# Blending a deformable-convolution sample: two VectorE operations in a row, one ScalarE scaling after them, and TensorE a tap later

## The chip, the cores and the metric

The kernel runs on one core of a Trainium2 chip. The metric is the device time of one execution in microseconds; the time before is the median of three runs. All profiles are of one execution of the kernel, recorded by the hardware profiler. The recorded execution is longer than the timed ones (7982.62 us against 7477.65 us), so shares and differences are read from the profile and times from the timed runs.

## The reference

Four images of 256 channels and 64x64 positions go through a normalisation over channels, three layers of modulated deformable 3x3 convolution with a ReLU each, a residual, and then a mixture of experts (two of eight for each token) with another residual. The change concerns the sampling in the deformable layers:

```python
y0 = jnp.floor(ys); x0 = jnp.floor(xs)
wy = (ys - y0)[:, None]; wx = (xs - x0)[:, None]
...
return v00 * (1 - wy) * (1 - wx) + v01 * (1 - wy) * wx + v10 * wy * (1 - wx) + v11 * wy * wx
...
sampled = _bilinear(x, ys, xs) * mask[:, None]      # mask = sigmoid(...)
out = jnp.einsum('bikhw,oik->bohw', sampled, wk) + b[None, :, None, None]
x = jax.nn.relu(out)                                 # three such layers
```

Each output position thus needs nine samples (the taps of the 3x3 kernel), each sample four neighbours weighted by the fractions wy and wx and by a mask.

## The kernel before

A table in DRAM holds for every position the row of 256 channel values and the difference to the row below it, so that one gather of 1024 numbers per position brings the left and the right column, each as (value, difference). The work goes in blocks of 512 positions: 4 groups of 128 positions (the partitions), times 9 taps, are 36 samples of 128x256. There are 96 blocks and so 3456 samples. For a tap `k` the loop treats the four groups in two pairs:

```python
def main_block(self, i, n, wins):
    ...
    acc = self.ps1.tile([P, CC, BLK], F32, tag="acc", ...)
    for k in range(K):
        sT = self.smT.tile([P, CC, BLK], F32, tag="sT", ...)
        for t0 in range(0, TPB, 2):
            tp = self.ps.tile([P, CC, 2 * P], F32, tag="tp", ...)
            gs, ss = [], []
            for t in (t0, t0 + 1):
                j = t * K + k
                g = self.gat.tile([P, 2, 2, C], F32, tag="g", ...)      # 10 buffers
                nc.gpsimd.indirect_dma_start(out=g..., in_=tb, in_offset=...)          # L445
                nc.vector.scalar_tensor_tensor(                                       # L451
                    g[:, :, 0, :], g[:, :, 1, :], cf[:, j, 0:1], g[:, :, 0, :], ALU.mult, ALU.add)
                s = self.smp.tile([P, C], F32, tag="s", ...)            # 6 buffers
                nc.scalar.activation(s, g[:, 0, 0, :], AF.Copy, scale=cf[:, j, 1:2])   # L456
                gs.append(g); ss.append(s)
            for u in range(2):
                j = (t0 + u) * K + k
                nc.vector.scalar_tensor_tensor(                                       # L461
                    ss[u], gs[u][:, 1, 0, :], cf[:, j, 2:3], ss[u], ALU.mult, ALU.add)
                for c in range(CC):
                    nc.tensor.transpose(tp[:, c, u*P:(u+1)*P], ss[u][:, c*P:(c+1)*P], self.ident)  # L465
            nc.scalar.copy(sT[:, :, t0 * P : (t0 + 2) * P], tp)                       # L470
        self.finish()                        # the matmuls of the tap before: acc += wk * sT  (L488)
        self.pend = (i, n, k, acc, sT, wins)
        self.step(k)                         # a piece of side work: tables, offsets, tokens
        self.pump()                          # a piece of the experts
```

L451 blends the rows of both columns at once (128x512 elements): value + wy * difference. L456 scales the left column by `(1 - wx) * mask` on ScalarE, and L461 adds the right column times `wx * mask` on VectorE. TensorE transposes the sample (L465), ScalarE copies the transposed pair from PSUM to SBUF (L470), and TensorE accumulates the tap (L488).

The three coefficients of a sample are made once for a block (the mask is `(1 + tanh)/2`):

```python
nc.vector.tensor_copy(cf[:, :, 0], fr[:, 0, :])                               # wy
for q, (s0, s1) in enumerate(((-0.5, 0.5), (0.5, 0.0))):
    hf = small(f"hf{q}", (P, J))
    nc.vector.tensor_scalar(hf, fr[:, 1, :], s0, s1, ALU.mult, ALU.add)       # (1-wx)/2, wx/2
    nc.vector.scalar_tensor_tensor(cf[:, :, 1 + q], th, 1.0, hf, ALU.add, ALU.mult)
```

The experts run beside the sampling: GpSimd's queue, which issues the gathers in order, also issues the load of an expert's weights (`w`, two buffers, L727) and of its tokens. The instructions of each engine are put in order by a scheduler when the program is built; an engine executes its own in that order.

Of the kernel before, what the change touches and what calls it, by code (L numbers as in the profile page):

```python
# [8 lines left out]
F32 = mybir.dt.float32  # L9
I32 = mybir.dt.int32  # L10
AF = mybir.ActivationFunctionType
ALU = mybir.AluOpType
AX = mybir.AxisListType

P = 128
H = W = 64
C = 256
CC = C // P
K = 9
NL = 3  # L20
TPB = 4
BLK = P * TPB
NB = H * W // BLK
RPB = BLK // W
J = TPB * K
# [10 lines left out]
FT = 1 << FT_LOG  # L36
FU = FT // P
GB = 10
WINN = CC * (RPB + 2) * (W + 2)
W1N = CC * HID + HC  # L40
W2N = HC * C + C
# [43 lines left out]
class Weave:  # L85
# [3 lines left out]
    def __init__(self, ctx, tc, ins, out):  # L89
        nc = self.nc = tc.nc  # L90
        self.tc = tc
        self.ins = ins
        self.x = ins["x"].rearrange("b (c p) h w -> b p c (h w)", p=P)
        self.out_v = out.rearrange("b (c p) h w -> b p c (h w)", p=P)
        self.B = self.x.shape[0]

        def pool(name, bufs, **kw):
            return ctx.enter_context(tc.tile_pool(name=name, bufs=bufs, **kw))

        self.cst = pool("cst", 1)  # L100
        self.dram = pool("dram", 1, space=bass.MemoryType.DRAM)
        self.wkp = pool("wkp", 1)
        self.plan = pool("plan", 22)
        self.win = pool("win", 3)
        self.wt = pool("wt", 2)
        self.small = pool("small", 1)
        self.big = pool("big", 2)
        self.ffn = pool("ffn", 2)
        self.rt = pool("rt", 1)
        self.rt2 = pool("rt2", 2)  # L110
        self.gyp = pool("gyp", 4)
        self.smT = pool("smT", 2)
        self.smp = pool("smp", 6)
        self.gat = pool("gat", GB)
        self.ps = pool("ps", 3, space=bass.MemoryType.PSUM)
        self.ps1 = pool("ps1", 1, space=bass.MemoryType.PSUM)
        self.queue = []
        self.credit = 0.0
        self.side = []
        self.tiles = []  # L120
        self.tile_credit = 0.0
        self.pend = None

# [108 lines left out]
    def window(self, n, nm, spare):  # L234

        if spare:
            if n % 2 == 0:
                self.pair = self.wt.tile([P, 2, WINN], F32, tag="wt", name=f"win_{nm}")
            w = self.pair[:, n % 2, :].rearrange("p (c r w) -> p c r w", c=CC, w=W + 2)
        else:  # L240
            w = self.win.tile([P, CC, RPB + 2, W + 2], F32, tag="win", name=f"win_{nm}")
        v = w.rearrange("p c r w -> p (c r) w")
        self.nc.vector.memset(v[:, :, 0 : W + 2 : W + 1], 0.0)
        if n == 0:
            self.nc.vector.memset(w[:, :, 0, 1 : W + 1], 0.0)
        if n == NB - 1:
            self.nc.vector.memset(w[:, :, RPB + 1, 1 : W + 1], 0.0)
        return w
# [61 lines left out]
    def off_block(self, l, b, n, w):  # L310

        nc = self.nc
        nm = f"{l}_{b}_{n}"
# [4 lines left out]
        for m, (k, c) in enumerate(terms):  # L318
            ky, kx = divmod(k, 3)
            g = m % NQ  # L320
# [22 lines left out]
        def small(tag, shape=(P, 2, J), dt=F32):  # L343
            return self.small.tile(list(shape), dt, tag=tag, name=f"{tag}_{nm}")

        idx = self.plan.tile([P, J], I32, tag="idx", name=f"idx_{nm}")
        cf = self.plan.tile([P, J, 3], F32, tag="cf", name=f"cf_{nm}")
        self.plans[l, b, n] = (idx, cf)

        th = small("th", (P, J))  # L350
# [22 lines left out]
        fr = small("fr")  # L373
# [5 lines left out]
        nc.vector.tensor_scalar(idx, ixf, float(TC + 1), None, ALU.add)  # L379
        yield  # L380

        nc.vector.tensor_copy(cf[:, :, 0], fr[:, 0, :])
        for q, (s0, s1) in enumerate(((-0.5, 0.5), (0.5, 0.0))):
            hf = small(f"hf{q}", (P, J))
            nc.vector.tensor_scalar(hf, fr[:, 1, :], s0, s1, ALU.mult, ALU.add)
            nc.vector.scalar_tensor_tensor(cf[:, :, 1 + q], th, 1.0, hf, ALU.add, ALU.mult)

    def pre_block(self, b, n, wins, spare):

# [38 lines left out]
        self.wk[k] = wk  # L428

    def main_block(self, i, n, wins):  # L430
        nc = self.nc
        l, b = self.stages[i]
        nm = f"{i}_{n}"
        idx, cf = self.plans.pop((l, b, n))
        tb = self.table(l, b)
        acc = self.ps1.tile([P, CC, BLK], F32, tag="acc", name=f"acc_{nm}")
        for k in range(K):
            sT = self.smT.tile([P, CC, BLK], F32, tag="sT", name=f"sT_{nm}_{k}")
            for t0 in range(0, TPB, 2):
                tp = self.ps.tile([P, CC, 2 * P], F32, tag="tp", name=f"tp_{nm}_{k}_{t0}")  # L440
                gs, ss = [], []
                for t in (t0, t0 + 1):
                    j = t * K + k
                    g = self.gat.tile([P, 2, 2, C], F32, tag="g", name=f"g_{nm}_{j}")
                    nc.gpsimd.indirect_dma_start(  # L445
                        out=g.rearrange("p x s f -> p (x s f)"),
                        out_offset=None,
                        in_=tb,
                        in_offset=bass.IndirectOffsetOnAxis(ap=idx[:, j : j + 1], axis=0),
                    )  # L450
                    nc.vector.scalar_tensor_tensor(  # L451
                        g[:, :, 0, :], g[:, :, 1, :], cf[:, j, 0:1], g[:, :, 0, :],
                        ALU.mult, ALU.add,
                    )
                    s = self.smp.tile([P, C], F32, tag="s", name=f"s_{nm}_{j}")
                    nc.scalar.activation(s, g[:, 0, 0, :], AF.Copy, scale=cf[:, j, 1:2])  # L456
                    gs.append(g)
                    ss.append(s)
                for u in range(2):
                    j = (t0 + u) * K + k  # L460
                    nc.vector.scalar_tensor_tensor(  # L461
                        ss[u], gs[u][:, 1, 0, :], cf[:, j, 2:3], ss[u], ALU.mult, ALU.add
                    )
                    for c in range(CC):
                        nc.tensor.transpose(  # L465
                            tp[:, c, u * P : (u + 1) * P],
                            ss[u][:, c * P : (c + 1) * P],
                            self.ident,
                        )
                nc.scalar.copy(sT[:, :, t0 * P : (t0 + 2) * P], tp)  # L470

            self.finish()
            self.pend = (i, n, k, acc, sT, wins)
            self.step(k)
            self.pump()

    def finish(self):

        if self.pend is None:
            return  # L480
        nc = self.nc
        i, n, k, acc, sT, wins = self.pend
        self.pend = None
        l, b = self.stages[i]
        nm = f"{i}_{n}"
        for o in range(CC):
            for c in range(CC):
                nc.tensor.matmul(  # L488
                    acc[:, o, :],
                    lhsT=self.wk[k][:, c, o * P : (o + 1) * P],  # L490
                    rhs=sT[:, c, :],
                    start=(k == 0 and c == 0),
                    stop=(k == K - 1 and c == CC - 1),
                )
        if n == NB - 1 and i + 1 < len(self.stages):
            self.load_tap(self.stages[i + 1][0], k, i + 1)
        if k < K - 1:
            return
        bk = self.bk[l]
        if l < NL - 1:  # L500
            w = wins[n] = self.window(n, nm, False)
            dst = [w[:, o, 1 : RPB + 1, 1 : W + 1] for o in range(CC)]
            src = [acc[:, o, :].rearrange("p (r w) -> p r w", w=W) for o in range(CC)]
        else:
            r = self.big.tile([P, CC, BLK], F32, tag="a", name=f"r_{nm}")
            dst = [r[:, o, :] for o in range(CC)]
            src = [acc[:, o, :] for o in range(CC)]
        nc.scalar.activation(dst[0], src[0], AF.Relu, bias=bk[:, 0:1])
        nc.vector.tensor_scalar(dst[1], src[1], bk[:, 1:2], 0.0, ALU.add, ALU.max)
        if l < NL - 1:  # L510
            self.rows_done(l + 1, b, n, wins)
        else:
            self.aside(5, self.tokens(b, n, r))
# [382 lines left out]
    def run(self):  # L896
# [14 lines left out]
        wins = {}  # L911
# [6 lines left out]
        for i, (l, b) in enumerate(self.stages):  # L918
            wins, pre = {}, {}
            for n in range(NB):  # L920
                self.main_block(i, n, wins)
                if i in beside:
                    self.aside(3, self.pre_block(beside[i], n, pre, i == 0))
            if i + 1 == len(self.stages) or self.stages[i + 1] == (l + 1, b):
                self.finish()
                self.settle()
        while self.queue or self.tiles:
# [49 lines left out]
```

## Time and profile before

| | |
|---|---|
| Time, median of 3 runs | 7477.65 us (7471.17 to 7482.62) |
| Span of the profiled execution | 7980.6 us, 92242 instructions |
| TensorE (PE) busy, mean granted clock | 6750.9 us (85%), 0.939 |
| VectorE (DVE) busy | 5033.4 us (63%) |
| ScalarE (ACT) busy | 3584.0 us (45%) |
| GpSimd (POOL) busy | 4536.3 us (57%) |
| DMA | 2210.66 MB, mean 277 GB/s; the gathers' queue takes 68.8% of 16 engines' span |

How to read it: busy time is the time in which an engine executes something; the rest is idle time, and the profile names for each idle stretch what ended it. [...] "PEld" is TensorE's weight load. In a line such as `A x <- B y: us, times, longest`, engine A stood still before an instruction that writes x until engine B had made y. "issue" is idle time for which the profile shows no other engine. From about 7400 us on there are no samples left, only experts and the final combination.

### The profile page before, as it was taken

Reading aid. Unit: us, or ns where it says so; the run is one execution under the profiler, and the core shown is the slowest. Engines: PE = TensorE matmul, PEld = TensorE weight load, DVE = VectorE, ACT = ScalarE, POOL = GpSimd, SP = SyncE. Lnnn points to the kernel's source line nnn. Section 1 sums busy time; section 2 is a strip of 40 time slices with the busy share of each in tenths; the row PEclk is TensorE's granted clock in tenths of the full one; section 3 lists DMA queues with packets and bytes.
Section 4 is the critical chain, followed back from the end, with each engine's and each line's share of the span. In section 5 each row is a group of like instructions: output and inputs, shape, how many; then the busy total and the mean of one; then the engine's idle time right before and its main releaser. Section 6 shows DMA issues by size and latency. Waiting matters only on the chain. (4 is left out here: it accounts for less than half of the span.)

```text
span 7980.6 us, 92242 instructions
## 1 busy us (share of the span) xinstructions
PE 6750.9 (85%) x27544; PEld 3696.8 (46%) x27544; DVE 5033.4 (63%) x11300; ACT 3584.0 (45%) x7355; POOL 4536.3 (57%) x4189
## 2 busy tenths in 40 slices
PE   6898888888988999988887899998888788888595
PEld 2444333334444445445543454444444444555374
DVE  4776777768886666666666666666666445556401
ACT  3554454445544444445543444445453333444121
POOL 1664666665656666655555566666555544555434
PEclk8999999999999999999988999999998889999697
DMA  4897999899987888887787898888887666767423
GB/s 148 312 330 279 328 321 338 315 325 329 357 307 275 298 305 314 304 306 268 277 294 267 282 316 303 292 307 300 285 298 248 233 233 233 274 248 285 133 94 119
DMA packets 751193, 2210.66 MB, mean 277 GB/s; under 512 B 105688, under 2 KB 206040, under 8 KB 746088
## 3 DMA queue, kind: packets, MB, share of 16 engines
q0 software_dynamic: 547392, 1929.26, 68.8%
q1 hardware_dynamic: 203304, 275.51, 10.2%
q8 instruction: 222, 3.64, 0.2%
q14 instruction: 275, 2.25, 0.1%
HBM read 2150.57 MB, written 195.61 MB: 294 GB/s over the span
## 5 line engine op out<-in xcount | busy, mean ns | idle before, releaser
L445 POOL DMA_INDIRECT g<-tab,idx x3456 | 3754.0, 1086 | 2382.0 <-DVE s L461 1219.3
L488 PE MATMUL acc<-sT,wk 128*128 128x512 f32 x6912 | 3502.4, 625 | 267.2 <-ACT sT L470 165.9
L461 DVE SCALAR_TENSOR_TENSOR s<-g,cf,s 128x256 f32<-128x256 f32 x3456 | 1623.6, 482 | 1669.9 <-ACT s L456 1271.3
L451 DVE SCALAR_TENSOR_TENSOR g<-g,cf 128x512 f32<-128x512 f32 x3456 | 2519.3, 744 | 236.9 <-DMA g<-tab,idx 194.1
L456 ACT ACTIVATE s<-g,cf 128x256 f32<-128x256 f32 x3456 | 1691.8, 509 | 1159.6 <-DVE g L451 903.7
L488 PEld LDWEIGHTS acc<-sT,wk 128*128 128x128 f32 x6912 | 1216.3, 198 | 1270.5 <-issue 894.2
L470 ACT COPY sT<-tp 128x512 f32<-128x512 f32 x1728 | 1003.8, 585 | 1678.0 <-PE tp L465 1178.7
L465 PE MATMUL tp<-ident,s 128*128 128x128 f32 x6912 | 1302.0, 286 | 427.2 <-DVE s L461 271.5
L465 PEld LDWEIGHTS tp<-ident,s 128*128 128x128 f32 x6912 | 877.4, 146 | 1659.4 <-issue 1008.6
L791 PE MATMUL py<-w,hT 128*128 128x256 f32 x2496 | 689.3, 398 | 123.8 <-ACT hT L785 88.6
L775 PE MATMUL ph<-fzT,w 128*128 128x256 f32 x2496 | 661.3, 395 | 59.8 <-ACT hT L785 20.6
L791 PEld LDWEIGHTS py<-w,hT 128*128 128x128 f32 x2496 | 447.0, 195 | 271.6 <-ACT hT L785 137.4
L727 POOL DMA_INDIRECT w<-in_W,wrow x156 | 175.8, 1127 | 693.2 <-issue 260.5
L775 PEld LDWEIGHTS ph<-fzT,w 128*128 128x128 f32 x2496 | 463.5, 197 | 184.4 <-issue 74.1
L785 ACT ACTIVATE hT<-ph,w 128x256 f32<-128x256 f32 x624 | 268.7, 471 | 538.1 <-PE ph L775 270.8
L321 PE MATMUL po<-win,wo 128*32 128x512 f32 x2304 | 464.1, 614 | 49.2 <-ACT win L256 33.0
L739 POOL DMA_INDIRECT zt<-z,tok x312 | 347.6, 1114 | 140.7 <-issue 85.6
L820 POOL DMA_INDIRECT gy<-ys,slots x256 | 257.7, 1007 | 219.4 <-DVE ta L828 105.1
L799 DVE TENSOR_TENSOR y<-py,w 128x512 f32<-128x512 f32 x156 | 107.5, 689 | 341.4 <-PE py L791 331.8
L291 ACT COPY hv<-tpv 128x512 f32<-128x512 f32 x384 | 210.5, 595 | 99.1 <-PE tpv L286 56.7
L321 PE MATMUL po<-win_pre,wo 128*32 128x512 f32 x1152 | 227.6, 640 | 17.7 <-ACT om L330 7.9
L828 DVE SCALAR_TENSOR_TENSOR ta<-gy,cw,ta 128x256 f32<-128x256 f32 x256 | 120.5, 482 | 125.4 <-DMA gy<-ys,slots 84.7
(151 smaller groups left out, 3621.4 us busy)
## 6 DMA issues: line engine op xcount, KB each, us to landing
tab<-hv SPq DMA_DIRECT2D x384, 256.0 KB
g<-tab,idx POOLq DMA_INDIRECT x3456
ys<-y SPq DMA_DIRECT2D x156, 256.0 KB
wk<-in_conv_w SPq DMA_DIRECT2D x108, 256.0 KB
xc_pre<-in_x SPq DMA_DIRECT2D x32, 512.0 KB
xr_tok<-in_x SPq DMA_DIRECT2D x32, 512.0 KB
t<-t_tok SPq DMA_DIRECT2D x32, 512.0 KB
ta<-t SPq DMA_DIRECT2D x64, 256.0 KB
```

What stands on the lines that cost most here:

```text
L321: nc.tensor.matmul(po[g * Q : (g + 1) * Q, :], lhsT=self.wo[l][:, k, c, :], rhs=w[:, c, ky : ky + RPB, kx : kx + W], start=(m < NQ), stop= ...
L445: nc.gpsimd.indirect_dma_start(out=g.rearrange("p x s f -> p (x s f)"), out_offset=None, in_=tb, in_offset=bass.IndirectOffsetOnAxis(ap=id ...
L451: nc.vector.scalar_tensor_tensor(g[:, :, 0, :], g[:, :, 1, :], cf[:, j, 0:1], g[:, :, 0, :], ALU.mult, ALU.add,)
L456: nc.scalar.activation(s, g[:, 0, 0, :], AF.Copy, scale=cf[:, j, 1:2])
L461: nc.vector.scalar_tensor_tensor(ss[u], gs[u][:, 1, 0, :], cf[:, j, 2:3], ss[u], ALU.mult, ALU.add)
L465: nc.tensor.transpose(tp[:, c, u * P : (u + 1) * P], ss[u][:, c * P : (c + 1) * P], self.ident,)
L470: nc.scalar.copy(sT[:, :, t0 * P : (t0 + 2) * P], tp)
L488: nc.tensor.matmul(acc[:, o, :], lhsT=self.wk[k][:, c, o * P : (o + 1) * P], rhs=sT[:, c, :], start=(k == 0 and c == 0), stop=(k == K - 1 ...
L739: self.nc.gpsimd.indirect_dma_start(out=zt, out_offset=None, in_=grp.zd, in_offset=bass.IndirectOffsetOnAxis(ap=grp.tok[:, j : j + 1], axi ...
L775: nc.tensor.matmul(ph[:, h, :], lhsT=w1[:, o : o + P], rhs=zT[:, c, :], start=(c == 0), stop=(c == CC - 1),)
L785: nc.scalar.activation(ht[:, h, :], ph[:, h, :], AF.Gelu, bias=w1[:, k : k + 1])
L791: nc.tensor.matmul(py[:, u, :], lhsT=hT[h // 2][:, h % 2, u * P : (u + 1) * P], rhs=w2[:, h * C : (h + 1) * C], start=(h == 0), stop=(h == ...
```

## The change

A sample becomes `((left + ratio * right)) * scale` with `ratio = wx / (1 - wx)` and `scale = (1 - wx) * mask`. VectorE then makes both blends one after the other without anything of ScalarE between them, and ScalarE's scaling comes last, in place. `1 - wx` is kept at or above 2^-30 so that the ratio stays finite. TensorE's part of a pair (its transposes, the copy of the result, and the tap's matmuls) is put two pairs (one tap) later in the program, and the samples have eight buffers instead of six. The purpose is that VectorE never has to wait in the middle of a sample, that the gather buffer is given back after two consecutive VectorE operations, and that TensorE finds its samples ready.

```diff
+LAG = 2
+LEAST = 2.0**-30
...
-        self.smp = pool("smp", 6)
+        self.smp = pool("smp", 8)
...
         nc.vector.tensor_copy(cf[:, :, 0], fr[:, 0, :])
-        for q, (s0, s1) in enumerate(((-0.5, 0.5), (0.5, 0.0))):
-            hf = small(f"hf{q}", (P, J))
-            nc.vector.tensor_scalar(hf, fr[:, 1, :], s0, s1, ALU.mult, ALU.add)
-            nc.vector.scalar_tensor_tensor(cf[:, :, 1 + q], th, 1.0, hf, ALU.add, ALU.mult)
+        left = small("left", (P, J))
+        nc.vector.tensor_scalar(left, fr[:, 1, :], -1.0, 1.0, ALU.mult, ALU.add)
+        nc.vector.tensor_scalar(left, left, LEAST, None, ALU.max)
+        inv = small("inv", (P, J))
+        nc.vector.reciprocal(inv, left)
+        nc.vector.tensor_tensor(cf[:, :, 1], fr[:, 1, :], inv, ALU.mult)
+        nc.vector.tensor_scalar(left, left, 0.5, None, ALU.mult)
+        nc.vector.scalar_tensor_tensor(cf[:, :, 2], th, 1.0, left, ALU.add, ALU.mult)
...
     def main_block(self, i, n, wins):
         for k in range(K):
             for t0 in range(0, TPB, 2):
+                ss = self.samples(i, n, k, t0, plan)
+                self.pairs.append((i, n, k, t0, wins, ss))
+                if len(self.pairs) > LAG:
+                    self.turn()
             self.step(k)
             self.pump()
...
+    def samples(self, i, n, k, t0, plan):            # for each of the two groups of a pair
+            nc.gpsimd.indirect_dma_start(...)                        # the gather, as before
+            nc.vector.scalar_tensor_tensor(                          # rows, as before
+                g[:, :, 0, :], g[:, :, 1, :], cf[:, j, 0:1], g[:, :, 0, :], ALU.mult, ALU.add)
+            s = self.smp.tile([P, C], F32, tag="s", ...)
+            nc.vector.scalar_tensor_tensor(                          # columns, by their ratio
+                s, g[:, 1, 0, :], cf[:, j, 1:2], g[:, 0, 0, :], ALU.mult, ALU.add)
+            nc.scalar.activation(s, s, AF.Copy, scale=cf[:, j, 2:3])
...
+    def turn(self):                                  # two pairs later
+        if t0 == 0:
+            self.sT = self.smT.tile([P, CC, BLK], F32, tag="sT", ...)
+        tp = self.ps.tile([P, CC, 2 * P], F32, tag="tp", ...)
+        # four transposes of ss into tp, as before
+        nc.scalar.copy(self.sT[:, :, t0 * P : (t0 + 2) * P], tp)
+        if t0 + 2 == TPB:
+            self.finish()
+            self.pend = (i, n, k, self.sT, wins)
...
     def finish(self):
+        if k == 0:
+            self.acc = self.ps1.tile([P, CC, BLK], F32, tag="acc", ...)
...
             if i + 1 == len(self.stages) or self.stages[i + 1] == (l + 1, b):
+                while self.pairs:
+                    self.turn()
                 self.finish()
                 self.settle()
```

## The prediction

> **What bounds the kernel now.** I read four views in this order: the costliest groups, the waits, a stretch of the timeline, and the busy time by stages. The groups first, to learn the price of one sample (3456 of them, each 128 positions by 256 channels):
>
> ```profile
> L445 POOL DMA_INDIRECT g<-tab,idx x3456 | 3754.0, 1086 | 2382.0 <-DVE s L461 1219.3
> L461 DVE SCALAR_TENSOR_TENSOR s<-g,cf,s 128x256 f32<-128x256 f32 x3456 | 1623.6, 482 | 1669.9 <-ACT s L456 1271.3
> L451 DVE SCALAR_TENSOR_TENSOR g<-g,cf 128x512 f32<-128x512 f32 x3456 | 2519.3, 744 | 236.9 <-DMA g<-tab,idx 194.1
> L456 ACT ACTIVATE s<-g,cf 128x256 f32<-128x256 f32 x3456 | 1691.8, 509 | 1159.6 <-DVE g L451 903.7
> ```
>
> After the bar stand busy time and mean ns, then the idle time before the group and what ended most of it. A sample goes DVE 744 ns, ACT 509 ns, DVE 482 ns. Of the 1670 us that VectorE is idle before the last step, 1271 end with the ScalarE scaling. The gathers' queue in turn is idle 1219 us until that last step gives a buffer back.
>
> The second view is VectorE's waits, because one wait decides whether data or arithmetic is late:
>
> ```profile
> DVE s L461 <- ACT s L456: 1271.3, 1247, 14.3
> DVE g L451 <- DMA g<-tab,idx: 194.1, 110, 9.2
> ```
>
> Columns: us in total, times, longest. Only 110 of 3456 first blends waited for their gather. So the rows are nearly always there before VectorE asks; what VectorE waits for is ScalarE, 1247 times.
>
> The third view is VectorE's timeline in a busy stretch:
>
> ```profile
> 3017.04 0.75 DVE L451 SCALAR_TENSOR_TENSOR g<-g,cf 128x512 f32<-128x512 f32 x1
> 3018.36 0.48 DVE L461 SCALAR_TENSOR_TENSOR s<-g,cf,s 128x256 f32<-128x256 f32 x1 [0.58 <-ACT s L456]
> 3018.76 0.75 DVE L451 SCALAR_TENSOR_TENSOR g<-g,cf 128x512 f32<-128x512 f32 x1
> ...
> 2461.00 0.23 DVE L370 TENSOR_TENSOR up<-pf,pos 128x72 f32<-128x72 f32 x1
> 2461.26 0.23 DVE L372 TENSOR_TENSOR fl<-pf,up 128x72 f32<-128x72 f32 x1
> ```
>
> From one L451 to the next is 1.72 us: 0.75 of blending, 0.58 of standing still while ScalarE scales, 0.48 of blending, less 0.08 of overlap (3018.76 lies before 3018.84). The last two lines give the price of two dependent VectorE operations in a row: 0.23 + 0.03 us from start to start. The overlap of 0.08 is lost and a gap of 0.03 appears, and no more.
>
> The fourth view is the busy time by stages (0 to 168 us is the lead-in):
>
> ```profile
> 168.00:2400.00 2232.00, 1934.79 (x7946) 928.75 (x7946) 1678.66 (x3828) 1122.67 (x2321) 1352.70 (x1225) 0.97 0.90 322
> 2400.00:6000.00 3600.00, 3166.85 (x12835) 1740.03 (x12834) 2363.54 (x5170) 1714.95 (x3519) 2191.58 (x2000) 0.95 0.84 294
> 6000.00:7400.00 1400.00, 1137.72 (x4454) 669.52 (x4452) 783.24 (x1660) 575.95 (x1168) 761.56 (x719) 0.91 0.71 251
> 7400.00:7980.00 580.00, 405.21 (x1704) 310.15 (x1702) 135.74 (x357) 110.73 (x238) 229.18 (x237) 0.79 0.36 112
> ```
>
> Columns: stretch, length, busy time of PE, PEld, DVE, ACT, POOL, then granted clock, DMA share, GB/s. The DMA engines are busy 0.90 of the time in the first stretch, 0.84 in the second, 0.71 in the third. They are the next limit and a near one: VectorE's serial step sets the pace, with the DMA 10 to 16% behind it. The page's best slice moved 357 GB/s, and 322/0.90 = 358, 294/0.84 = 350: I take some 355 GB/s as what a full share moves in this mix.
>
> [...]
>
> **The change part by part.**
>
> *Order within a sample.* Still three operations of the same sizes, but VectorE's two stand next to each other; the changed program's order of instructions shows them adjacent nearly throughout. A serial sample costs VectorE 0.745 + 0.03 + 0.48 - 0.08 = 1.18 us instead of 1.72. Pairs that the scheduler had already interleaved (two first blends, then two second ones) cost 0.66 + 0.40 = 1.06 and now also cost 1.18. The waits say that 1247 samples stood; their stall of 1271 us goes, and the rest lose up to 2209 x 0.12 = 265 us. Net, VectorE's own chain becomes some 1000 us shorter. That cannot all appear as time, because the DMA is close behind.
>
> *Release of the gather buffer.* It was held for first blend, scaling and second blend (1.8 us at the least), now for 1.2 us, so gathers are issued sooner from the ten buffers.
>
> *The lag of two pairs.* TensorE's transposes of a pair come after the samples of two further pairs. TensorE waited 271 us (matmuls) and 363 us (weight loads) for the second blend; most of this should go. ScalarE stands before the copy of sT until the transposes end (1179 us); that used to hold up the scaling behind it, and through it VectorE. With eight sample buffers VectorE may run four pairs ahead, so that wait no longer reaches it. Cost: one tap of extra latency where the pairs are drained at a few stage ends, some 6 us each, tens of us at most.
>
> *Coefficients.* Four small operations per block become six, dependent ones. At some 0.2 us each, two more and the lost overlap make about 0.6 us x 96 blocks = 60 us of VectorE, which then has idle time to hold them.
>
> *The sum.* In the first stretch (no experts) the DMA share should rise from 0.90 to about 0.95: 2232 x 0.90/0.95 = 2114, 118 us less. In the second, from 0.84 to 0.91: 3600 x 0.84/0.91 = 3323, 277 less. In the third, GpSimd's queue is held by loads of expert weights, and gathers wait behind them whatever VectorE does; 0.71 to 0.74 gives 57 less. The lead-in and the tail from 7400 on have no samples: nothing. Together 452 of 7981 us, 5.7%. The unprofiled time is 7477.65; the same share of it is 424 us, so about 7050 us. The shares 0.95, 0.91 and 0.74 are my choice: nothing in the profile says how close to full the DMA comes when ten buffers are returned without stalls, only that slices with a digit of 9 exist.
>
> **The rivals.** (a) *The DMA hides it all.* If the transfers had been the true limit, shortening VectorE's step would only turn 1271 us of waiting on ScalarE into waiting on data. For: the shares 0.90 and 0.84. Against: only 110 waits for data now. It would leave about 7400. (b) *TensorE becomes the bound.* Per tap it has eight matmul passes and eight transposes, which in dense bursts take 0.43 and 0.11 us each, 4.3 us a tap, plus convolution of offsets and experts; the accumulation still waits for the copy of the tap's last transposes (166 + 298 us now). For: in the middle stretch it has the most work. Against: [...] PE waits on ScalarE and VectorE today. It would leave about 7200 to 7250. (c) *Full gain.* The DMA reaches 0.97 in both main stretches: 161 + 482 us, plus 57, are 700 profiled, 656 unprofiled, 6820. (d) *A loss.* ScalarE's queue now holds the scaling as the last link before TensorE, behind copies that wait for TensorE. If the lag is not enough, TensorE waits for ScalarE more than it did for VectorE, clock falls, and the time is at or above 7480. The eight buffers and the extra tap speak against it.
>
> **Range and chances.** I expect between (a) and (c), with the weight on a gain that the DMA cuts to about half of the freed time: 7050, with 6820 to 7300 for 8 in 10. Two per cent faster means below 7328. I give 0.86 to that, 0.10 to within 2%, 0.04 to slower.
>
> **What would show it.** Right: the wait of the second blend on ScalarE gone from the head of the list; VectorE pairs 0.78 us from start to start; VectorE now waiting for gathers hundreds of us; the gathers' queue waiting less for the second blend; DMA share and GB/s up in the first two stretches; PE clock up. Wrong: first blends still rarely waiting for data while the second blend waits on sample buffers (TensorE), or TensorE's transposes waiting on the scaling for more than the 634 us that they waited for the second blend; either would mean that the limit was downstream of VectorE. A third stretch that shrinks as much as the others would show that I have taken the weight loads for too firm a limit.

## The result and the profile after

The changed kernel takes 7310.85 us (median of 4 runs, 7305.9 to 7321.0), the kernel before 7480.14 us (median of 4). The ratio is 0.9773, with a 95% interval of 0.9754 to 0.9793: 169 us or 2.3% less. The span of the profiled execution is 7319.2 us.

The groups first (busy time and mean ns, then the idle time before the group and what ended it):

```profile
L458 POOL DMA_INDIRECT g<-tab,idx x3456 | 3617.3, 1047 | 2222.1 <-DVE s L469 860.6 <-issue 589.0 <-DVE inv L390 165.3
L464 DVE SCALAR_TENSOR_TENSOR g<-g,cf 128x512 f32<-128x512 f32 x3456 | 2560.1, 744 | 305.2 <-DMA g<-tab,idx 248.7 <-issue 31.8 <-PE po L323 21.7
L472 ACT ACTIVATE s<-s,cf 128x256 f32<-128x256 f32 x3456 | 1690.1, 509 | 952.4 <-DVE s L469 917.6 <-DVE mv_pre L60 10.9 <-DVE left L388 6.5
L469 DVE SCALAR_TENSOR_TENSOR s<-g,cf 128x256 f32<-128x256 f32 x3456 | 1655.0, 482 | 241.6 <-PE po L323 20.9 <-issue 6.2 <-DVE g L464 3.8
```

The prices are what they were (744, 482, 509 ns), and VectorE stands idle before the second blend for 241.6 us in all. The profile that the prediction was made from had 1669.9 us there; a record of the kernel before that fits the timed runs has 1207.8 (run 1 below). The change did to VectorE what it was made for. The waits (us in total, times, longest) show TensorE's side:

```profile
ACT sT L490 <- PE tp L487: 1392.2, 1173, 7.8
PEld tp L487 <- ACT s L472: 728.5, 1488, 9.6
DVE g L464 <- DMA g<-tab,idx: 248.7, 224, 9.5
PE tp L487 <- ACT s L472: 142.4, 291, 9.5
```

TensorE's transposes now wait for ScalarE's scaling: the weight loads (PEld) for 728.5 us, the matmuls (PE) for 142.4. The two must not be added up as lost time: of the 728.5 us, some 581 lie under matmuls that are running. VectorE's waits for gathers, which I had expected to grow to hundreds of us more, are 249. The third view is VectorE's timeline in a busy stretch (start us, us):

```profile
3014.06 0.75 DVE L464 SCALAR_TENSOR_TENSOR g<-g,cf 128x512 f32<-128x512 f32 x1
3014.84 0.48 DVE L469 SCALAR_TENSOR_TENSOR s<-g,cf 128x256 f32<-128x256 f32 x1
3015.24 0.75 DVE L464 SCALAR_TENSOR_TENSOR g<-g,cf 128x512 f32<-128x512 f32 x1
```

From first to second blend are 0.78 us and from sample to sample 1.18 us: both as predicted. The stages (length, busy time of PE, PEld, DVE, ACT, POOL, granted clock, DMA share, GB/s):

```profile
168.00:2400.00 2232.00, 2002.89 (x8420) 989.17 (x8421) 1792.52 (x4094) 1167.89 (x2460) 1402.87 (x1305) 0.98 0.91 340
2400.00:6000.00 3600.00, 3324.92 (x13921) 1868.16 (x13919) 2594.20 (x5671) 1816.58 (x3754) 2277.85 (x2193) 0.98 0.89 317
```

The DMA share is 0.91 where I had put 0.95, and 0.89 where I had put 0.91. TensorE is busy 2002.89/2232 = 0.90 and 3324.92/3600 = 0.92 of these stretches.

### The profile page after: what moved, and what is told of

Read it like the earlier page. It is cut to its first block, busy times and chain, and to the rows that moved or that the text cites. A ratio compares the mean times of both kernels' runs of the same rounds, so it can differ in the third digit from the quotient of the medians.

```text
span 7319.2 us, 90081 instructions
## 1 busy us (share of the span) xinstructions
PE 6531.9 (89%) x27544; PEld 3635.1 (50%) x27544; DVE 5116.8 (70%) x11492; ACT 3550.5 (49%) x7352; POOL 4352.3 (59%) x4189
## 5 line engine op out<-in xcount | busy, mean ns | idle before, releaser
L458 POOL DMA_INDIRECT g<-tab,idx x3456 | 3617.3, 1047 | 2222.1 <-DVE s L469 860.6
L510 PE MATMUL acc<-sT,wk 128*128 128x512 f32 x6912 | 3416.2, 609 | 170.3 <-ACT sT L490 165.1
L464 DVE SCALAR_TENSOR_TENSOR g<-g,cf 128x512 f32<-128x512 f32 x3456 | 2560.1, 744 | 305.2 <-DMA g<-tab,idx 248.7
L472 ACT ACTIVATE s<-s,cf 128x256 f32<-128x256 f32 x3456 | 1690.1, 509 | 952.4 <-DVE s L469 917.6
L469 DVE SCALAR_TENSOR_TENSOR s<-g,cf 128x256 f32<-128x256 f32 x3456 | 1655.0, 482 | 241.6 <-PE po L323 20.9
L510 PEld LDWEIGHTS acc<-sT,wk 128*128 128x128 f32 x6912 | 1177.4, 193 | 1061.6 <-issue 685.9
L487 PEld LDWEIGHTS tp<-ident,s 128*128 128x128 f32 x6912 | 883.0, 145 | 1376.6 <-ACT s L472 728.5
L487 PE MATMUL tp<-ident,s 128*128 128x128 f32 x6912 | 1301.9, 285 | 151.9 <-ACT s L472 142.4
L813 PE MATMUL py<-w,hT 128*128 128x256 f32 x2496 | 647.2, 388 | 37.2 <-ACT hT L807 36.4
L797 PE MATMUL ph<-fzT,w 128*128 128x256 f32 x2496 | 630.2, 384 | 19.4 <-ACT fzT L789 15.0
L821 DVE TENSOR_TENSOR y<-py,w 128x512 f32<-128x512 f32 x156 | 107.6, 690 | 595.2 <-PE py L813 594.5
L761 POOL DMA_INDIRECT zt<-z,tok x312 | 310.1, 994 | 164.1 <-issue 85.4
L856 PE MATMUL otp<-ident,ta 128*128 128x128 f32 x256 | 72.7, 385 | 177.2 <-DVE ta L850 102.1
```

Source lines behind the costliest of these rows:

```text
L458: nc.gpsimd.indirect_dma_start(out=g.rearrange("p x s f -> p (x s f)"), out_offset=None, in_=self.table(*self.stages[i]), in_offset=bass.I ...
L464: nc.vector.scalar_tensor_tensor(g[:, :, 0, :], g[:, :, 1, :], cf[:, j, 0:1], g[:, :, 0, :], ALU.mult, ALU.add,)
L469: nc.vector.scalar_tensor_tensor(s, g[:, 1, 0, :], cf[:, j, 1:2], g[:, 0, 0, :], ALU.mult, ALU.add)
L472: nc.scalar.activation(s, s, AF.Copy, scale=cf[:, j, 2:3])
L487: nc.tensor.transpose(tp[:, c, u * P : (u + 1) * P], ss[u][:, c * P : (c + 1) * P], self.ident)
L510: nc.tensor.matmul(acc[:, o, :], lhsT=self.wk[k][:, c, o * P : (o + 1) * P], rhs=sT[:, c, :], start=(k == 0 and c == 0), stop=(k == K - 1 ...
```

## The experiments

Chips differ: the kernel before takes 7480 to 7490 us on some and 8050 to 8062 us on others, so every ratio below is to the kernel before on the same chip in the same series. "Kind A" is the first and "kind B" the second. Runs 1 to 4, 17 and 18 come from chips of kind A (the result too by its times; its chip is not on record), runs 5 to 16 from three chips of kind B. No chip was used in two series, so it is not shown whether the kind belongs to the chip or to a condition that lasted through a series.

### 1. The kernel before, recorded again

No edit. The profile that I predicted from spans 7980.6 us, while the timed runs took 7477.65.

> The kernel before, unchanged, profiled once more. Its recorded execution was 7982.6 us and its timed ones 7480, while the changed kernel's recorded execution (7321) is as long as its timed ones (7311). Theory R (the recorder stretched that one execution, with stalls that the timed runs don't have, so the sum of the prediction was taken from a stretched record): this record is again 300 us or more above its timed runs, or it comes out near 7480 with clearly fewer us of waits of the second blend on ScalarE than 1271. Theory S (the record was faithful in its shares): the same 1271 us within 10% whatever the span.

Measured: 7487.71 us, ratio 0.9996 [0.9985, 1.0007], span of the recorded run 7495.0. So recording did not stretch this run. The profile that I worked from is taken to be one of a chip of kind B, and the times of one of kind A: its chip is not on record, but its late signals of TensorE (668 us against 8 here; the section on runs 5 to 9 explains them) are those of kind B, and its span lies within about 1% of the times there. The wait of the second blend is nearly the same on both, 1184.5 us against 1271, which is what theory S said. The waits of this record that the change bears on:

```profile
DVE s L461 <- ACT s L456: 1184.5, 1587, 4.7
PEld tp L465 <- DVE s L461: 432.3, 712, 4.4
PE tp L465 <- DVE s L461: 276.3, 296, 10.5
```

So TensorE's matmuls wait for samples 142.4 us after the change and 276.3 before it; its weight loads wait longer, but mostly under running matmuls. The stages on the chip of kind A:

```profile
168.00:2400.00 2232.00, 1961.51 (x8134) 947.04 (x8135) 1721.82 (x3916) 1154.26 (x2386) 1397.77 (x1261) 0.98 0.92 331
2400.00:6000.00 3600.00, 3294.95 (x13609) 1822.90 (x13608) 2505.93 (x5496) 1794.60 (x3680) 2348.15 (x2150) 0.97 0.88 311
```

Here the DMA share is 0.92 and 0.88 before the change already, not 0.90 and 0.84, and TensorE is busy 0.88 and 0.92. There was less room than the record had shown. What the changed order brought to VectorE's queue is seen in its other waits, of this kernel and then of the changed one:

```profile
DVE y L799 <- PE py L791: 327.0, 91, 17.1
DVE pos L356 <- ACT th L351: 63.0, 63, 6.1
DVE win L509 <- ACT win L508: 55.4, 38, 5.7
```

```profile
DVE y L821 <- PE py L813: 594.5, 108, 16.7
DVE pos L358 <- ACT th L353: 234.1, 77, 9.1
DVE win L531 <- ACT win L530: 226.2, 55, 8.9
```

All three are side work in VectorE's queue that needs something of TensorE or ScalarE: an expert's result, the offsets, a stage's output. VectorE now runs ahead and stands there: (594.5 + 234.1 + 226.2) - (327.0 + 63.0 + 55.4) = 609 us more. That is most of what was freed: before the second blend 1207.8 - 241.6 = 966 us of idle time are gone, but VectorE's idle time as a whole fell only from 7495.0 - 5039.3 = 2455.7 to 7319.2 - 5116.8 = 2202.4 us, by 253.

### 2 and 3. One half of the change at a time (kind A)

Run 2 keeps the order of the blends and takes the lag away; run 3 keeps the lag and the eight buffers with the old blend.

```diff
-LAG = 2                                  # run 2, against the changed kernel
+LAG = 0
-        self.smp = pool("smp", 8)
+        self.smp = pool("smp", 6)
```
```diff
             s = self.smp.tile(...)       # run 3, against the changed kernel (old coefficients too)
+            nc.scalar.activation(s, g[:, 0, 0, :], AF.Copy, scale=cf[:, j, 1:2])
+        for u in range(2):
             nc.vector.scalar_tensor_tensor(
-                s, g[:, 1, 0, :], cf[:, j, 1:2], g[:, 0, 0, :], ALU.mult, ALU.add)
-            nc.scalar.activation(s, s, AF.Copy, scale=cf[:, j, 2:3])
+                ss[u], gs[u][:, 1, 0, :], cf[:, j, 2:3], ss[u], ALU.mult, ALU.add)
```

> The changed blend (two VectorE operations, then ScalarE) but no lag (LAG = 0) and six sample buffers as before. If the serial step DVE-ACT-DVE was the limit, this alone gives most of the 170 us: 7320 to 7370. If TensorE and its neighbours are the limit, the sample still reaches TensorE after three operations and TensorE still stands before each pair: 7430 to 7500, or slower than before, because ScalarE's in-order queue now has the scaling as the last link.

> The old blend (VectorE, ScalarE, VectorE) with the lag of two pairs and eight sample buffers. If the serial step was the limit, no more than 40 us of gain: 7440 to 7490. If TensorE waiting for its samples was the limit, most of the 170 us: 7310 to 7370.

Measured: order alone 7396.62 us, 0.988 [0.9863, 0.9896]; lag alone 7363.16 us, 0.9837 [0.9818, 0.9856]. Each half is worth 1.2% and 1.6%, together 2.3%: most of what either does remains beside the other. Run 3 is where I had put the case that TensorE waiting for its samples was the limit (7310 to 7370); run 2 lies between its two ranges. The waits, of run 2 and then of run 3:

```profile
PE tp L487 <- ACT s L472: 223.6, 363, 9.0
```

```profile
DVE s L470 <- ACT s L465: 1234.6, 1639, 5.4
PE tp L486 <- DVE s L470: 177.6, 226, 10.4
```

In run 3 VectorE still stands in the middle of its samples as long as before (1234.6 us against 1184.5), and yet the time falls by 1.6%: so the serial step alone did not set the pace. The wait of TensorE's matmuls for samples goes with the time in these runs: 276.3 us at 7487.71, 223.6 at 7396.62, 177.6 at 7363.16 and 142.4 at 7310.85.

### 4. Half of the gathers (kind A)

One gather serves both samples of a pair; 906 MB of 2211 and half of the sampled data are left out.

```diff
-            g = self.gat.tile(...); nc.gpsimd.indirect_dma_start(...)
+            if t == t0:
+                g = self.gat.tile(...); nc.gpsimd.indirect_dma_start(...)
```

> The changed kernel with one gather for each pair of samples: the second sample of a pair blends the first one's buffer again, so the output is wrong by that, and 1728 of 3456 gathers (906 MB) are left out, with every operation of VectorE, ScalarE and TensorE kept. If the DMA limits the changed kernel (rival a), the time falls by several hundred us, to 6600 to 6900. If TensorE or VectorE limits it, it falls by less than 150 us, to 7160 or more.

Measured: 7430.21 us, 0.9913 [0.9894, 0.9932]: slower than the changed kernel with 41% less traffic. It does not decide the question, because the edit also moved instructions: up to ten first blends stand ahead of their second blends in VectorE's order (nearly always one in the changed kernel), and VectorE waited for data more, not less:

```profile
POOL g L459 <- DVE s L470: 2473.3, 1165, 14.7
DVE g L465 <- DMA g<-tab,idx: 1296.8, 902, 7.3
```

It shows only that the bytes alone do not set the time. Whether the DMA binds the changed kernel on a chip of kind A was tested by no other run; against it speaks that VectorE's waits for gathers did not grow (272.4 us in run 1, 248.7 after).

### 5 to 9. What chips of kind B do

Run 9 is the changed kernel unchanged, as the reference. Run 5 adds a write of 226 MB (a tenth of the traffic) whose data nothing reads, though VectorE waits for the sample buffers that it holds (79 times, 152.7 us); run 6 leaves half of the accumulation matmuls out, run 8 does so in the kernel before; run 7 leaves the second blend out, and ScalarE scales from the gather buffer.

```diff
+        nc.sync.dma_start(self.extra[(t0 // 2 + k) % 4], ss[0])          # run 5
```
```diff
         for o in range(CC):                                              # runs 6 and 8
-            for c in range(CC):
+            for c in range(1):
```
```diff
-            nc.vector.scalar_tensor_tensor(                              # run 7
-                s, g[:, 1, 0, :], cf[:, j, 1:2], g[:, 0, 0, :], ALU.mult, ALU.add)
-            nc.scalar.activation(s, s, AF.Copy, scale=cf[:, j, 2:3])
+            nc.scalar.activation(s, g[:, 0, 0, :], AF.Copy, scale=cf[:, j, 2:3])
```

> The changed kernel with one more transfer of 128 KB for each pair of samples (the pair's first sample is also written to DRAM): 226 MB on top of 2211, 10% more, nothing of the computation altered, and VectorE's order of instructions stays as it is. If the DMA limits the kernel (rival a), 4 to 8% slower than the changed kernel's 7311: 7600 to 7900. If it doesn't, below 7400.

> The changed kernel with half of the accumulation left out (only the first 128 input channels of each tap are multiplied): 3456 matmul passes of 0.43 us, 1480 us of TensorE, are gone, everything else stays. If TensorE (with what stands in VectorE's and ScalarE's queues waiting for it) limits the changed kernel, it falls by 300 us or more, below 7000. If the DMA or VectorE limits it, 7150 to 7300.

> The changed kernel without the second blend (ScalarE scales the left column straight from the gather buffer, the right column is left out): 3456 VectorE operations, some 1390 us of VectorE at 0.40 us each, are gone. If VectorE's own work limits the changed kernel, below 7000. If not, 7200 to 7320.

> The kernel before with the same half of the accumulation left out. If the serial step of VectorE and ScalarE was the limit before, as predicted, the time hardly moves: 7400 or more. If TensorE limited it already then, below 7150.

> The changed kernel unchanged, as the control for the three that follow, and to see its ratio to the kernel before on this chip: 0.977 where the kernel before takes 7480 us; if the kernel before takes some 8050 us here, either the same 0.977, or, if the gain depends on how often TensorE falls to half its clock, another ratio by 2% or more.

Measured: run 9 takes 8908.45 us, ratio 1.104 [1.0997, 1.1083]. The change that gains 2.3% on a chip of kind A loses 10% on one of kind B. Run 5: 8951.15 us, 1.1094 [1.1061, 1.1128], so a tenth more traffic is nearly free there and the DMA is not what binds. Run 7: 7963.89 us, 0.9881 [0.9854, 0.9908]: without the second blend the loss is gone. Runs 6 and 8 have less TensorE work and became slower, which none of my cases foresaw: 9021.13 us, 1.1194 [1.1158, 1.1231], and 8327.11 us, 1.0328 [1.0301, 1.0355].

The timeline of run 9 shows how the time is lost (start us, us; in brackets the idle time before and what ended it):

```profile
2740.26 0.38 PE L487 MATMUL tp<-ident,s 128*128 128x128 f32 x2
...
2741.43 1.05 PE L323 MATMUL po<-win,wo 128*32 128x512 f32 x2
...
2744.06 0.48 DVE L469 SCALAR_TENSOR_TENSOR s<-g,cf 128x256 f32<-128x256 f32 x1
...
2750.03 0.94 POOL L458 DMA_INDIRECT g<-tab,idx  x1 [0.30 <-issue]
2754.08 0.59 ACT L490 COPY sT<-tp 128x512 f32<-128x512 f32 x1 [17.24 <-remote]
...
2755.12 0.69 PE L487 MATMUL tp<-ident,s 128*128 128x128 f32 x2 [12.64 <-ACT s L472]
```

ScalarE stands 17.24 us before the copy of two transposes whose last matmuls are recorded at 2740.26 to 2740.64. "remote" means that the semaphore was raised just before the start, with no instruction found that ended then: TensorE's signal came at 2754.00, 13.4 us after the recorded end. Meanwhile VectorE fills the sample buffers and stops, GpSimd issues gathers until it has no buffer left, and the scaling that TensorE needs next stands behind the copy: it starts at 2754.56, though the last blend had ended at 2744.54. No packet of the two queues that the profile calls instruction (q8 and q14) starts between 2724.33 and 2763.91 us, so the pause does not look like a load of instructions. The windows around it (columns as above) show the clock following:

```profile
2730.00:2742.00 12.00, 11.94 (x45) 6.22 (x43) 8.53 (x16) 3.50 (x7) 9.26 (x10) 1.00 0.97 340
2742.50:2747.20 4.70, 0.00 (x0) 0.00 (x0) 1.78 (x4) 0.00 (x0) 3.79 (x4) 1.00 1.01 409
2747.30:2754.00 6.70, 0.00 (x0) 0.00 (x0) 0.00 (x0) 0.00 (x0) 2.82 (x3) 0.50 1.03 412
2754.00:2760.80 6.80, 5.64 (x14) 3.87 (x15) 0.00 (x0) 3.82 (x9) 0.00 (x0) 0.50 0.15 61
2761.20:2770.00 8.80, 8.80 (x37) 5.65 (x35) 4.86 (x8) 3.87 (x10) 1.21 (x1) 1.00 0.00 1
```

First the pause, then half clock until 6.8 us after it, and after it the DMA engines run dry, because nothing was blended and no buffer came back. To count it I compared each rise of TensorE's semaphore with the recorded end of the last instruction before it that raises it, and summed those more than 1.5 us late, beside the time at half clock:

| kernel, chip | time us | TensorE's signals late, us | at half clock, us |
|---|---|---|---|
| before, A (run 1) | 7488 | 8 | 604 |
| changed, A | 7311 | 8 | 546 |
| before, B (the profile predicted from) | 8050 | 668 | 981 |
| changed, B (run 9) | 8908 | 2316 | 1961 |
| changed, more DMA, B (5) | 8951 | 2029 | 1996 |
| changed, half accumulation, B (6) | 9021 | 1876 | 3470 |
| changed, no second blend, B (7) | 7964 | 1012 | 1001 |
| before, half accumulation, B (8) | 8327 | 456 | 2805 |
| order alone, B (13) | 8815 | 1917 | 1720 |
| lag alone, B (14) | 7913 | 788 | 1020 |

The signals of VectorE and ScalarE are not late on either kind. (The times for chips of kind B are medians of the timed runs; for the kernel before, of the series of run 9. In records of chips of kind B semaphore events of TensorE, VectorE and ScalarE are missing, in the one predicted from 17, 22 and 23% of them, in that of the changed kernel on kind A none; a missing event can hide a late signal, but not make one. It also leaves more idle time without a named cause: before the second blend 254.1 us in the record predicted from, 11.4 in run 1.)

### 10 to 12. VectorE's wait for y, and a shorter lag (kind B)

Run 10 puts the expert's result `y` one part of the expert later in the program. Run 11 makes `y` from the weights, so that VectorE does not wait for TensorE there (its values mean nothing then). Run 12 sets the lag to one pair.

```diff
+        yield                                             # run 10; an expert has 4 parts, not 3
         y = self.ffn.tile([P, FU, C], F32, tag="y", ...)
```
```diff
-            y, py, w2[:, HC * C :]...                     # run 11
+            y, w2[:, : FU * C]..., w2[:, HC * C :]...
```
```diff
-LAG = 2                                                   # run 12
+LAG = 1
```

> The changed kernel with VectorE's expert addition y put one quarter of an expert's step after the matmuls that it reads (four parts of an expert for three). Theory V (VectorE's in-order queue, now ahead of TensorE, stands before side work that TensorE has not made yet: 595 us before y against 327 in the kernel before): the wait before y falls by half or more and the time by 1 to 3%. Theory D (the DMA is what is left): within 0.5% of the changed kernel.

> The changed kernel with y made from the expert's weights in SBUF instead of TensorE's result (the experts' output is left out of the answer; the same VectorE operation of the same size, without the wait for TensorE). Theory V: 2 to 5% faster than the changed kernel. Theory D: within 0.5%.

> The changed kernel with a lag of one pair instead of two. Theory V: VectorE's head start over TensorE is smaller, the waits before y, pos and win are smaller, and the time is the same or lower (up to 1%). If the head start is what brings the gain, half of the lag's part is lost: 0.5% slower than the changed kernel.

Measured: 8866.48 us (1.0996 [1.0959, 1.1033]), 8823.0 (1.0938 [1.0899, 1.0977]) and 8896.63 (1.1051 [1.1009, 1.1094]), against 1.104 for run 9. Run 10 did not do what it was made for: the wait before `y` rose to 1130.6 us, from 926.6 in run 9. Leaving the wait for TensorE out altogether is worth 1%, less than the 2 to 5% of theory V (VectorE then waits 343.7 us for the weights instead); one pair of lag or two is the same. None of this is where 10% go.

### 13 to 16. Which half loses on kind B

The kernels of runs 2, 3, 11 and 10 again. They fell to a third chip of kind B.

> The change without its lag and with six sample buffers: the order blend, blend, scale alone. Where the kernel before takes some 7480 us this measured 0.988 of it; where the kernel before takes some 8050 us the whole change measured 1.104. If the scaling on ScalarE as the last link before TensorE is what costs there, this kernel costs most of it too: 1.06 to 1.12 on such a chip. If it is the lag with its denser stream, this kernel stays at 0.98 to 1.02 there.

> The old blend (scaling between the two VectorE operations) with TensorE two pairs later and eight sample buffers. On a chip of the kind with 7480 us before: 0.984 as measured. On one with 8050 us before: 1.06 to 1.12 if the lag is what costs there, 0.98 to 1.02 if it is the order of the blends.

> The changed kernel, but the expert's result y is made from the weights in SBUF instead of from TensorE's product in PSUM (its values are then meaningless): VectorE no longer waits there. If the waits of VectorE's queue for TensorE's side work gave back what the blends freed, the 595 us that stood before y are worth 100 us or more: 7150 to 7210 where the changed kernel takes 7311, and 85 us as it measured where that one takes 8908. If VectorE's waits are only a symptom of TensorE's pace, the gain is under 40 us.

> The changed kernel with y one part of the expert later in the program, which should do by order what the run without the wait does by leaving it out, with the right values. Where the changed kernel takes 7311 us: 7200 to 7260 if these waits bind, 7300 to 7330 if they are a symptom.

Measured: order alone 8814.89 us, 1.0937 [1.0898, 1.0976]; lag alone 7913.22 us, 0.9793 [0.9751, 0.9836]. This settles which half: the order of the blends makes the loss, and the lag gains about the same on both kinds of chip. It does not say how the order does it. ScalarE's waits for a late signal of TensorE, order alone first, then lag alone:

```profile
ACT sT L490 <- remote: 777.2, 143, 14.1
```

```profile
ACT sT L489 <- remote: 199.6, 60, 9.5
```

Runs 15 and 16 gave 8810.63 us (1.0919 [1.0884, 1.0953]) and 8888.1 us (1.1028 [1.0992, 1.1064]): as before, 1% and little (in run 16 the wait before `y` was 1120.9 us, again not shorter). What the wait for `y` is worth on a chip of kind A was not tried.

### 17 and 18. ScalarE beside the path, and another buffer (kind A)

In run 17 ScalarE scales into a buffer that nobody reads, and TensorE takes the blended sample itself: the factor is left out of the result, while every engine does the same amount of work. In run 18 the second blend stays in the gather buffer and ScalarE scales from there.

```diff
-            nc.scalar.activation(s, s, AF.Copy, scale=cf[:, j, 2:3])     # run 17
+            d = self.smd.tile([P, C], F32, tag="d", ...)                 # one buffer; smp has 7
+            nc.scalar.activation(d, s, AF.Copy, scale=cf[:, j, 2:3])
```
```diff
-                s, g[:, 1, 0, :], cf[:, j, 1:2], g[:, 0, 0, :], ALU.mult, ALU.add    # run 18
-            nc.scalar.activation(s, s, AF.Copy, scale=cf[:, j, 2:3])
+                g[:, 0, 0, :], g[:, 1, 0, :], cf[:, j, 1:2], g[:, 0, 0, :], ALU.mult, ALU.add
+            nc.scalar.activation(s, g[:, 0, 0, :], AF.Copy, scale=cf[:, j, 2:3])
```

> The changed kernel, with ScalarE's scaling done beside the path: it writes to a buffer that nobody reads, and TensorE takes the sample as VectorE left it (the factor is left out of the result; all engines do the same amount of work; seven sample buffers instead of eight). If the last link over ScalarE is what costs where the kernel before takes 8050 us, this falls from 1.10 to 0.96 to 1.02 there, and the late signals of TensorE (over 1.5 us: 2316 us in the changed kernel, 668 before) fall under 1000 us. If VectorE's denser pairs are what disturbs TensorE, it stays at 1.08 to 1.11. Where the kernel before takes 7480 us: 7150 to 7230 if TensorE's 871 us of waiting for the scaling bind, 7290 to 7330 if not.

> The changed kernel, with the second blend written back into the gather buffer and ScalarE scaling from there into the sample buffer; the values are the right ones. The gather buffer is held for one step more, but VectorE needs no sample buffer, so it cannot be stopped by TensorE directly. Where the kernel before takes 8050 us: 0.97 to 1.03 if the in-place scaling or VectorE's waiting for sample buffers is what costs, 1.08 to 1.11 if it is the order of the three operations as such. Where it takes 7480 us: 7280 to 7400, since gathers return later.

Measured: 7267.59 us, 0.9696 [0.968, 0.9713], and 7307.3 us, 0.9758 [0.9742, 0.9775]. The waits of run 17:

```profile
PEld tp L489 <- DVE s L470: 192.8, 365, 2.1
PE tp L489 <- DVE s L470: 85.4, 98, 9.1
```

The matmuls' wait for samples falls from 142.4 to 85.4 us, the weight loads' from 728.5 to 192.8, and the time falls by about 40 us (7267.59 against 7310.85, and against 7307.3 of run 18 on the same chip). So ScalarE as the last link costs about 0.6% on a chip of kind A: real, but between my two expectations, and a small part of what was missing. It fits the 57 us of the matmuls and not the 536 of the weight loads, which mostly wait while matmuls run. Run 18 equals the changed kernel: which buffer is written made no difference on a chip of kind A (7307.3 us against 7310.85). On one of kind B, where it mattered, neither of the two was run.

## Why the prediction was wrong

*VectorE's step: right.* The pair takes 0.78 us from start to start, a sample 1.18, and the wait of the second blend on ScalarE (1184.5 us in run 1) left the list.

*The step that failed is the sum, and under it the premise that "VectorE's serial step sets the pace, with the DMA 10 to 16% behind it".* From it I took the DMA share as the only thing that cuts the freed time ("from 0.84 to 0.91"). Runs 2 and 3 contradict the premise: with VectorE's serial wait left whole the time fell by 1.6% (run 3), with the wait removed and nothing else by 1.2% (run 2). With both, 966 us of that wait gone, the span of the changed kernel is only 7495.0 - 7319.2 = 176 us shorter. The sum has two faults. The first is its starting point. The shares 0.90 and 0.84 are those of kind B; on the chips on which the change was timed they were 0.92 and 0.88 (run 1). The same targets from there give 2232 x (1 - 0.92/0.95) = 70 us and 3600 x (1 - 0.88/0.91) = 119 us, 189 in place of 395. That this comes near the measured gain is luck: the targets were my choice, and the shares reached were others (0.91 and 0.89). I had seen that the recorded run was 500 us longer than the timed ones and scaled it by a percentage, as if recording had stretched it evenly. The second fault is that TensorE was left out of the sum: I had set its 85% aside, though no view showed how much more it could take, and asked nothing further. The 395 us, scaled to the timed run as I did it, are 370. Taking them out of 5832 us of kind A asks TensorE to do its work of the two stretches, 1961.51 + 3294.95 us, in 5462 us: a busy share of 0.96, above the 0.90 and 0.92 that the changed kernel reached.

*Where the freed time went.* Of the 966 us of idle time that vanished before VectorE's second blend, 713 came back elsewhere in its queue on the chip of kind A, 609 of them before `y`, `pos` and `win`. These are places where its queue has caught up with TensorE and ScalarE. TensorE itself, which is busy 88% of the span before and 89% after, lost little idle time: 7495.0 - 6613.7 = 881 us before, 7319.2 - 6531.9 = 787 after. One of my signs was ill chosen: transposes waiting on the scaling for more than 634 us were to mean a limit downstream of VectorE. They wait 728.5 + 142.4 = 871 us (before, on kind A, 432.3 + 276.3 = 709), but such a sum counts loads that wait under running matmuls; the matmuls' own wait was halved. Run 3 and the places where VectorE now stands point to a limit downstream. No run on a chip of kind A took work from TensorE, so that TensorE is the bound there is what the busy shares suggest, not what is shown.

*By stages.* The three stretches of the sum end at gathers 1223, 2926 and 3456 of the record that I used. Between the starts of the same gathers on kind A, run 1 took 2174, 3375 and 1203 us, the changed kernel 2105, 3303 and 1155: 69, 71 and 48 us less, where I had put 118, 277 and 57. So the term that was most wrong is the middle stretch, 277 us for 71. The last one was nearly right in size, though by a share of 4.0% it shrank more than the others (3.2% and 2.1%), which by my own sign means that I took the loads of expert weights for too firm a limit.

*The release of the gather buffer: small.* On the same kind of chip the gathers' queue waited 1064.1 us for the second blend before and 860.6 after.

*The lag: right in sign.* Alone it gives 1.6% on kind A and 2.1% on kind B, and the wait of TensorE's matmuls for the second blend, most of which was to go, fell by about a third on kind A (276.3 to 177.6 us); with both halves, where the scaling has taken the second blend's place, it is 142.4.

*The rivals.* (a) In its time (7400) and its sign (VectorE waiting on data) wrong. (b) The nearest on the chip of kind A, though its 7200 to 7250 were still too low. (c) Wrong. (d) named the link that would suffer, ScalarE's scaling behind copies that wait for TensorE; on a chip of kind A this costs about 40 us. On a chip of kind B the loss was real, 10.4%, and it goes with pauses of TensorE that no rival contained.

## What to carry to other kernels

Before a gain is worked out from a recorded run, its span is to be held against the timed runs: where they differ by almost 7%, the record may be of another chip, and its waits and shares are not those of the timed kernel. When a wait is removed from one engine, work out the busy share that the new time would ask of each other engine, and look for the next instruction in the freed engine's queue that needs one of them (here the wait for `y` grew from 327.0 to 594.5 us). A wait of weight loads that lay under running matmuls was not lost time of TensorE here: 536 us less of it in run 17 came with some 40 us less time. One reordering can be worth 2% on one chip and cost 10% on another; here the lag (a consumer moved a step later, with more buffers) gained on both, 0.9837 and 0.9793, and is the part to keep if both kinds of chip must run it.

## What was not expected of the hardware

*Two kinds of chip.* The same program took 7480 to 7490 us on some chips and 8050 to 8062 on three others. The durations of single VectorE and ScalarE instructions (744, 482, 509 ns) agree on both within 2 ns (742, 481 and 508 in run 9). The difference that the records show is in TensorE: late signals of 668 us against 8 for the kernel before, and more half clock, 981 us against 604. In run 9 signals more than 4 us late came 229 times, up to 28.6 us. Most of them lie in times of full DMA (median share 1.01 during such a pause, against 0.88 over all windows of 2 us), as in the windows shown, but the changed kernel on a chip of kind A has as much full DMA (the median over all windows of 2 us is 0.98) and late signals of 8 us in all, and a tenth more traffic did not lengthen them (2029 us in run 5, 2316 in run 9). Why the order of the blends triples them is open. That ScalarE is the last link before TensorE is not enough by itself: run 7 has that as well, with less VectorE work, and takes 0.988.

*Less TensorE work, slower clock.* The records show TensorE at two values of the granted clock, full and half. In the one predicted from, the 981 us at half clock lie in 135 pieces: 77 last 3.4 us, 37 last 6.8, 12 last 10.2, and the other nine longer. In the windows of run 9 half clock came after 4.7 us of standstill. But it also comes with little standstill: in run 8 TensorE stood still for more than 3.4 us, the commonest length of a piece, only 49 times (285 us together) and yet ran 2805 us at half clock, in 414 pieces. The mean clock was 0.832 there, against 0.939 in the record predicted from, and the accumulation matmul took 802 ns against 625:

```profile
L488 PE MATMUL acc<-sT,wk 128*128 128x512 f32 x3456 | 2328.2, 802 | 373.1 <-ACT sT L470 244.0 <-issue 114.3 <-DVE g L451 4.1
```

Half of these matmuls were left out, and the kernel became 3.3% slower. The clock does not account for that alone: TensorE's busy time fell from 6750.9 to 6162.6 us, but its idle time grew from 1230 to 2186 us. Why is open.
